# Layer 3's row sums, its last block, and the layout of loads and stores in a four-layer kernel

## The chip, the cores and the metric

The kernel runs on one core of a Trainium2 chip. A core has a matrix engine (TensorE, PE in the profile; its weight loads are listed as PEld), a vector engine (VectorE, DVE), a scalar engine (ScalarE, ACT), a general engine (GpSimd, POOL) and a queue processor (SyncE, SP). TensorE reads the on-chip memory SBUF, which has 128 partitions, and writes the accumulators in PSUM. SP, ScalarE and GpSimd can issue DMAs; these run on 16 DMA engines that all queues share. The metric is the time of one execution on the device in microseconds (us), the median of several runs.

## The reference

The input `x` has four images of 64 x 64 positions with 64 channels, all float32. Four layers follow one another; each keeps the shape.

```python
# layer 0: attention over the 4096 positions of an image, applied transposed
attn = softmax(q @ k.T);  x = gamma * (attn.T @ v) + x
# layer 1: norm, 1x1 conv to 256, 3x3 depthwise conv, y1*y2, channel attention, 1x1 conv, add;
#          norm, 1x1 conv to 256, z1*z2, 1x1 conv, add
# layer 2: x is read as (B, C, H, W) though it is (B, H, W, C); N = 4096
attn = softmax(xf.T @ xf);  x = (xf @ attn.T) + x
# layer 3: attention with 32 inner channels
f = softmax(theta_x @ phi_x.T);  w_y = (f @ g_x) @ w_W + w_b
mean, var = w_y.mean((0, 1, 2)), w_y.var((0, 1, 2))      # over all four images
x = x + gamma * (w_y - mean) * rsqrt(var + 1e-3) + beta
```

Layer 3's softmax needs, for each of 4096 queries, a sum of exponentials over 4096 keys; and its normalisation needs the statistics of all four images before any output can be written.

## The kernel before, in words

`fast_path` does the work; at its end a count of row sums outside a safe range (`bad`) decides whether `general_path` is run instead, and here it isn't.

**Layout.** An image is kept as `X[:, b]`, 128 x 2048: the partition is 64 x (parity of the column) + channel, and the free index runs over 32 column pairs with 64 rows h in each. A load brings rows h into partitions and 128 values (two columns of 64 channels) into each of eight blocks q, then TensorE transposes the blocks (`load_x`, L886). The view of the loads and stores is `by_rows = "h (q p w) c -> p h q (w c)"` (L733): column = 4q + 2p + w, so that one piece that is contiguous in memory is two columns, 512 bytes. Each image takes four loads (`g` and `p`, L744) of 256 KB, all on SP, and four stores (L1445), all on SP.

**Order of the work.** TensorE, ScalarE and VectorE run in an order written out by hand (`tc.manual_schedule`, `run()`). A list `items` holds the score steps, in turn layer 0 of all images (32 items each), then layer 2 of image 0, layer 2 of image 1, layer 3 of image 0, and so on; layer 3 of image 3 (`layer3(B - 1)`) is last. `due` holds what has to follow an item by so many items. Two lanes, `conv` (layer 1) and `misc` (projections, loads, closing steps), put generator steps between the items by a table of estimated times. What stands after `run()`, the normalisation and the stores, isn't under the manual schedule: the scheduler places it, each engine still executing its own list in order.

**Layer 3** handles an image in two halves of 32 items. In item n, `scores` makes a 128-key by 2048-query block of scores with four row groups of TensorE (L1284) into two PSUM tiles, and ScalarE writes the exponentials to `e` (L1289), one of six buffers. Two items later, `products` multiplies `e` by `gx` with four column groups (L1297), and the same `e` is added to the row sums in one of two ways:

```python
            if mc % 10 == 9:
...
                for k in range(4):
                    mm(
                        st["z"][32 * k : 32 * k + 32, :], ones[:, 0:32], e[:, bass.ts(k, 512)],
                        start=mc == 9, stop=False,
                    )
            elif mc == 1:
                nc.vector.tensor_add(esum, es[n - 1], e)
            elif mc:
                nc.vector.tensor_add(esum, esum, e)
```

TensorE sums over the key partitions with a matrix of ones (L1305) for the blocks 9, 19 and 29 of a half, VectorE adds the other blocks elementwise (L1310, L1312). At the end of a half, `totals` brings VectorE's sum through the ones into the same accumulator `z` (L1320), copies `z` to SBUF on ScalarE (L1324), takes its reciprocal (L1325) and scales the products (L1326) on VectorE. `close` multiplies by the output weights (L1336), adds the bias on ScalarE (L1338), gathers statistics in `bst` (L1340) and the extremes of the reciprocals (L1342) for the safe-range check. A float32 matmul stands in the trace as two passes, so a group of four is eight records.

**The end.** After the last half, the statistics are aggregated (L1412); TensorE averages the mean over the two parities with the matrix `half` (L1414), VectorE forms squared differences (L1418 to L1420), TensorE averages these (L1421), and a few one-column instructions give scale and shift (L1423 to L1428). Eight output tiles follow: scale and shift on ScalarE (L1434), add to `X` on VectorE (L1435), eight transposes (L1438), copies by VectorE and ScalarE (L1442, L1443), two stores (L1445). Then the flag `bad` is read by every engine and the kernel closes.

**The start.** While SP loads the images, GpSimd loads the weights, and ScalarE's queue loads 28 small vectors into `rows` and `gam` (L805, L810, L824), which TensorE turns into columns (L816) ahead of the first projection.

Of the kernel before, what the change touches and what calls it, by code (L numbers as in the profile page):

```python
# [691 lines left out]
def fast_path(ctx: ExitStack, tc: tile.TileContext, a: dict, out: bass.AP, bad):  # L692
# [42 lines left out]
    by_rows = "h (q p w) c -> p h q (w c)"  # L735
    rows_x = []
    for b in range(B):
        if b % 2 == 0:
            both = new_big("xr")
        t = both[:, bass.ts(b % 2, 2048)].rearrange("p (q n) -> p q n", n=128)  # L740
        src = a["x"][b].rearrange(by_rows, p=2, w=2)
        for g in range(2):
            for p in range(2):
                nc.sync.dma_start(  # L744
                    out=t[64 * p : 64 * p + 64, bass.ts(g, 8)], in_=src[p, :, bass.ts(g, 8)]
                )
        rows_x.append(t)
# [22 lines left out]
    ones = const.tile([128, 64], F32, name="ones")  # L770
# [109 lines left out]
    bst = const.tile([128, B, 2, 2, 6], F32, name="bst")  # L880
# [176 lines left out]
    def layer1(b):  # L1057
# [5 lines left out]
        for r in (1, 0):  # L1063
# [6 lines left out]
            inner = pad[:, PW + 1 : 65 * PW + 1].rearrange("p (q s h) -> p q s h", s=2, h=PW)  # L1070
            for j in range(4):
# [6 lines left out]
                for s in range(2):  # L1078
                    act(  # L1079
                        inner[:, bass.ts(j, 8), s, 0:H],  # L1080
                        ps[:, bass.ts(s, 512)].rearrange("p (q h) -> p q h", h=H),
                        AF.Identity, bias=pwb[:, 0, r : r + 1],
                    )
# [27 lines left out]
        for j in range(4):  # L1111
            ps = new_ps()
            for s in range(2):
                w0 = 16 * j + s
                mm(
                    ps[64 * s : 64 * s + 64, 0:512], pw2s, yg[:, w0 : w0 + 15 : 2, :],
                    start=True, stop=True,
                )
# [155 lines left out]
    def layer3(b):  # L1274
        m, first = im[b], len(items)
# [15 lines left out]
        def products(n):  # L1291
# [9 lines left out]
            if mc % 10 == 9:  # L1301
                if mc == 9:
                    st["z"] = new_acc("accz")
                for k in range(4):
                    mm(  # L1305
                        st["z"][32 * k : 32 * k + 32, :], ones[:, 0:32], e[:, bass.ts(k, 512)],
                        start=mc == 9, stop=False,
# [9 lines left out]
        def totals():  # L1317
# [6 lines left out]
            nc.scalar.copy(yz[:, 512:1024], z)  # L1324
            nc.vector.reciprocal(yz[:, 512:1024], yz[:, 512:1024])  # L1325
            nc.vector.tensor_mul(yz[:, 0:512], yz[:, 0:512], yz[:, 512:1024])  # L1326

        def close(nb):
# [6 lines left out]
            for jj in range(2):  # L1335
                mm(ps[:, bass.ts(jj, 512)], wo[jj], yz[:, 0:512], start=True, stop=True)  # L1336
            wy = wys[b][:, bass.ts(nb, 1024)]
            act(wy, ps, AF.Identity, bias=V("L3_conv_w_b"))  # L1338
            for i in range(2):
                nc.vector.bn_stats(bst[:, b, nb, i, :], wy[:, bass.ts(i, 512)])  # L1340
# [64 lines left out]
    half = new_t("half")[:, 0:128]  # L1405
    for i in range(2):
        nc.vector.tensor_scalar_mul(half[:, 64 * i : 64 * i + 64], ident[:, 0:64], 0.5)
    for i in range(2):
        cols = slice(64 * i, 64 * i + 64)
        stt(half[:, cols], ident[:, 64:128], 0.5, half[:, cols], ALU.mult, ALU.add)  # L1410
# [3 lines left out]
    mm(ps[:, 0:1], half, mv[:, 0:1], start=True, stop=True)  # L1414
    mean = sm.tile([128, 1], F32, tag="mean", name="mean")
    nc.vector.tensor_copy(mean, ps[:, 0:1])
    dm = sm.tile([128, 1], F32, tag="dm", name="dm")
    nc.vector.tensor_sub(dm, mv[:, 0:1], mean)  # L1418
    nc.vector.tensor_mul(dm, dm, dm)
    nc.vector.tensor_add(dm, dm, mv[:, 1:2])  # L1420
    mm(ps[:, 512:513], half, dm, start=True, stop=True)  # L1421
    scale = sm.tile([128, 1], F32, tag="scale", name="scale")
    act(scale, ps[:, 512:513], AF.Sqrt, bias=eps3)  # L1423
# [3 lines left out]
    nc.vector.tensor_mul(shift, scale, mean)  # L1427
    nc.vector.tensor_sub(shift, V("L3_conv_beta"), shift)  # L1428
    for b in range(B):
        dst = out[b].rearrange(by_rows, p=2, w=2)  # L1430
        for g in range(2):
# [12 lines left out]
            for p in range(2):  # L1444
                nc.sync.dma_start(  # L1445
# [72 lines left out]
```

## Time and profile before

| what | value |
|---|---|
| median of 3 runs | 2860.71 us (2859.96 to 2860.85) |
| the profiled execution: its own time | 2859.4 us |
| its span, first to last instruction | 2857.6 us |
| TensorE busy | 2756.5 us, 96% |
| ScalarE busy | 1751.3 us, 61% |
| VectorE busy | 1443.8 us, 51% |
| ones for row sums, L1305 | 192 records (24 groups) |
| adds for row sums, L1312 and L1310 | 216 x 2.29 us and 8 x 2.29 us |
| loads of x, stores of out | 16 and 16, 256 KB each, 4.7 and 4.6 us to landing |

The profile is one execution of the program. A row of a group of instructions names the line, the engine, the operation, and output and input tiles; "x8" is the number of instructions, and the time beside a row of the order in time is from the first start to the last end. TensorE overlaps its instructions, so the length of one record is more than what it adds to a stream. A wait names the instruction that ended it. The chain lists what ended last, followed back from the end.

### The profile page before, as it was taken

The numbers are of one execution on the slowest core, as the hardware profiler recorded it, in microseconds if no ns is written. First come the engines' busy times: TensorE is split into PE (matmuls) and PEld (weight loads), VectorE is DVE, ScalarE is ACT, GpSimd is POOL, SyncE is SP. The second block draws the span as 40 slices with busy tenths as digits, with TensorE's granted clock in tenths as the row PEclk, the third lists the DMA queues.
The fourth block names the chain that finished last, engine by engine and source line by source line (L and its number), as shares of the span: only waits on it lengthen the run. The fifth ranks groups of instructions, "written<-read, shape, count | busy, mean of one in ns | idle before, by whom it ended". The sixth has DMA issues, their size and how long they took to land.

```text
span 2857.6 us, 41692 instructions
## 1 busy us (share of the span) xinstructions
PE 2756.5 (96%) x17976; PEld 933.6 (33%) x17976; DVE 1443.8 (51%) x1548; ACT 1751.3 (61%) x2815; POOL 25.0 (1%) x85
## 2 busy tenths in 40 slices
PE   6999999999999999989999999999999999999995
PEld 3333333333333333322333332243322333322222
DVE  2322386633875438622673118930058610198996
ACT  3555555556465555655655558855678756578884
POOL 3000000000000000000000000000000000000000
PEclk9999999999999999999999999999999999999997
DMA  3000000000000000000000000000000000000002
GB/s 70 1 1 1 0 1 1 1 0 1 1 1 1 1 0 1 1 1 1 1 1 1 1 1 1 1 1 1 1 1 1 1 1 1 1 1 1 1 1 60
DMA packets 18460, 11.86 MB, mean 4 GB/s; under 512 B 1300, under 2 KB 18141, under 8 KB 18269
## 3 DMA queue, kind: packets, MB, share of 16 engines
q1 hardware_dynamic: 16896, 8.39, 1.4%
q8 instruction: 142, 2.33, 0.3%
q0 software_dynamic: 1120, 0.72, 0.2%
q14 instruction: 49, 0.40, 0.0%
q10 hardware_dynamic: 253, 0.02, 0.0%
HBM read 4.94 MB, written 4.19 MB: 3 GB/s over the span
## 4 chain that ended last, share of the span: by engine, by line
PE 91%; DVE 5%; ACT 3%; issue 1%; POOL 0%; DMA 0%; ACTq 0%; DVEq 0%; POOLq 0%
PE acc L1007 16%; PE ps L983 16%; PE acc L1194 16%; PE ps L1177 15%; PE ps L1284 9%; PE acc L1297 8%; PE ps L1131 2%; PE ps L1074 1%; PE ps L1031 1%; ACT e L1289 1%; DVE yz L1325 1%; PE ps L1336 1%; PE accz L1305 1%; DVE tg L1312 1%; PE var L1040 1%
## 5 line engine op out<-in xcount | busy, mean ns | idle before, releaser
L987 ACT ACTIVATE e<-ps 128x1024 f32<-128x1024 f32 x512 | 516.8, 1025 | 325.2 <-PE ps L983 201.0
L1185 ACT ACTIVATE e<-ps 128x1024 f32<-128x1024 f32 x512 | 517.0, 1024 | 315.4 <-PE ps L1177 314.9
L1289 ACT ACTIVATE e<-ps 128x1024 f32<-128x1024 f32 x512 | 496.1, 1023 | 110.2 <-PE ps L1284 92.4
L1312 DVE TENSOR_TENSOR tg<-tg,e 128x2048 f32<-128x2048 f32 x216 | 495.0, 2292 | 27.2 <-ACT e L1289 8.5
L983 PE MATMUL ps<-kv,q 64*128 64x512 f32 x2048 | 491.4, 607 | 11.9 <-ACT e L987 3.9
L1177 PE MATMUL ps<-ko 64*64 64x512 f32 x4096 | 473.9, 595 | 18.1 <-ACT ko L1160 8.7
L1194 PE MATMUL acc<-e,X 64*64 64x512 f32 x4096 | 467.7, 591 | 0.6 <-ACT yz L1315 0.6
L1007 PE MATMUL acc<-e,vq 128*64 128x512 f32 x2048 | 467.3, 598 | 0.0
L1014 DVE SCALAR_TENSOR_TENSOR X<-acc,gam,X 128x512 f32<-128x512 f32 x256 | 191.3, 749 | 276.8 <-PE acc L1007 263.9
L1284 PE MATMUL ps<-tg,ph 32*128 32x512 f32 x2048 | 320.3, 640 | 5.6 <-ACT e L1289 4.2
L983 PEld LDWEIGHTS ps<-kv,q 64*128 64x128 f32 x2048 | 189.1, 186 | 293.4 <-issue 187.6
L1297 PE MATMUL acc<-e,tg 128*32 128x512 f32 x2048 | 272.7, 605 | 1.3 <-ACT yz L1315 1.3
L1177 PEld LDWEIGHTS ps<-ko 64*64 64x64 f32 x4096 | 152.4, 133 | 313.7 <-issue 196.4
L1194 PEld LDWEIGHTS acc<-e,X 64*64 64x64 f32 x4096 | 156.9, 133 | 281.5 <-issue 271.3
L1007 PEld LDWEIGHTS acc<-e,vq 128*64 128x64 f32 x2048 | 136.3, 136 | 311.9 <-issue 289.9
L1202 DVE TENSOR_TENSOR ph<-ph,acc 128x512 f32<-128x512 f32 x16 | 11.0, 688 | 387.6 <-ACT ph L1201 387.6
L1284 PEld LDWEIGHTS ps<-tg,ph 32*128 32x128 f32 x2048 | 102.3, 183 | 223.6 <-issue 149.0
L1096 DVE SCALAR_TENSOR_TENSOR y<-pad,vec,y 128x1024 f32<-128x1024 f32 x128 | 164.3, 1283 | 7.6 <-ACT pad L1079 3.5
L1096 DVE SCALAR_TENSOR_TENSOR yg<-pad,vec,yg 128x1024 f32<-128x1024 f32 x128 | 164.3, 1284 | 3.8
L987 ACT ACTIVATION_READ_ACCUMULATOR e<-ps 128x1 f32 x512 | 106.5, 208 | 0.0
L1185 ACT ACTIVATION_READ_ACCUMULATOR e<-ps 128x1 f32 x512 | 105.9, 207 | 0.0
L1297 PEld LDWEIGHTS acc<-e,tg 128*32 128x32 f32 x2048 | 41.0, 108 | 196.4 <-issue 190.6
(173 smaller groups left out, 1229.2 us busy)
## 6 DMA issues: line engine op xcount, KB each, us to landing
xr<-in_x_dram SPq DMA_DIRECT2D x16, 256.0 KB, 4.7
out_dram<-o SPq DMA_DIRECT2D x16, 256.0 KB, 4.6
pw<-in_L_conv_pw_w_dram POOLq DMA_DIRECT2D x4, 64.0 KB, 4.2
phw<-in_L_conv_phi_W_dram POOLq DMA_DIRECT2D x8, 8.0 KB, 3.7
wq<-in_L_conv_Wq_dram POOLq DMA_DIRECT2D x4, 16.0 KB, 6.6
sca<-in_L_conv_sca_w_dram POOLq DMA_DIRECT2D x1, 64.0 KB, 3.8
pw<-in_L_conv_pw_w_dram POOLq DMA_DIRECT2D x2, 32.0 KB, 4.0
thw<-in_L_conv_theta_W_dram POOLq DMA_DIRECT2D x4, 8.0 KB, 3.7
```

What stands on the lines that cost most here:

```text
L983: mm(ps[:, bass.ts(r, 512)], m.q[rows_, bass.ts(t, 128)], m.k[rows_, bass.ts(g, 512)], start=True, stop=True,)
L987: act(es[g // 2][:, bass.ts(g % 2, 1024)], ps, AF.Exp, bias=SHIFT0, accum_out=zs[:, g : g + 1],)
L1007: mm(accs[g][64 * r : 64 * r + 64, :], vq, es[half][:, 1024 * g + 512 * r : 1024 * g + 512 * r + 512], start=t == 2 * p, stop=t == 2 * p + 1,)
L1014: stt(xs, accs[g], gam0, xs, ALU.mult, ALU.add)
L1096: stt(out_, win, wt, out_, ALU.mult, ALU.add)
L1177: mm(ps[64 * c : 64 * c + 64, bass.ts(r, 512)], m.ko[rows_, 128 * jb + 64 * c : 128 * jb + 64 * c + 64], m.ko[rows_, bass.ts(2 * ib + r, 5 ...
L1185: act(es[n, jb], ps, AF.Exp, bias=SHIFT2, accum_out=m.zs[:, jb, ib : ib + 1])
L1194: mm(acc[r][64 * c : 64 * c + 64, :], xw[rows_, jb, :], es[n, jb][rows_, bass.ts(c, 512)], start=jb == 0, stop=jb == 31,)
L1284: mm(tiles[k // 2][:, bass.ts(k % 2, 512)], m.ph[rows_, bass.ts(mc, 128)], m.th[rows_, bass.ts(nb, 512)], start=True, stop=True,)
L1289: act(e[:, bass.ts(kp, 1024)], tiles[kp], AF.Exp)
L1297: mm(st["y"][32 * k : 32 * k + 32, :], m.gx[:, mc, :], e[:, bass.ts(k, 512)], start=mc == 0, stop=mc == 31,)
L1312: nc.vector.tensor_add(esum, esum, e)
```

## The change

The diff has five parts.

- **Row sums.** A half's blocks 5, 11, 17, 23 and 29 go to TensorE's ones in place of 9, 19 and 29; in the last image's second half the blocks 30 and 31 (items 62 and 63) go there too.
- **The closing of a half.** Reciprocal and multiply are done in two pieces of 256 columns; the output matmul, the bias and the statistics follow by pieces as well, so that `bst` has twice the entries. For the last image the reciprocal reads the accumulator in PSUM directly, with no copy by ScalarE.
- **The statistics.** The variance over the two parities comes from half their sum and half their difference: `half` gets a second part, two matmuls are issued together, and the second round of TensorE is left out.
- **Layout.** The column is 32p + 2q + w, so that eight blocks q of one p are contiguous in memory, 4 KB for each row h. The depthwise convolution needs the true column order, so the writes into `pad` (L1079) and the reads of `yg` (L1115) are permuted. The other layers treat positions alike whatever their order.
- **Stores.** Those of p = 0 stay on SP, those of p = 1 are issued from GpSimd.

```diff
--- before.py
+++ after.py
@@ -732,13 +732,13 @@
 
 
     X = keep.tile([128, B, 2048], F32, name="X")
-    by_rows = "h (q p w) c -> p h q (w c)"
+    by_rows = "h (p q w) c -> p h q (w c)"
     rows_x = []
     for b in range(B):
         if b % 2 == 0:
             both = new_big("xr")
         t = both[:, bass.ts(b % 2, 2048)].rearrange("p (q n) -> p q n", n=128)
-        src = a["x"][b].rearrange(by_rows, p=2, w=2)
+        src = a["x"][b].rearrange(by_rows, p=2, q=16)
         for g in range(2):
             for p in range(2):
                 nc.sync.dma_start(
@@ -767,7 +767,7 @@
     nc.gpsimd.memset(eps1, EPS1)
     eps3 = const.tile([128, 1], F32, name="eps3")
     nc.gpsimd.memset(eps3, EPS3)
-    ones = const.tile([128, 64], F32, name="ones")
+    ones = const.tile([128, 32], F32, name="ones")
     nc.gpsimd.memset(ones, 1.0)
 
     def blocks(nm, weight, n_out, places, width):
@@ -877,7 +877,7 @@
     sums0 = const.tile([128, B, 32], F32, name="sums0")
     sums2 = const.tile([128, B, 32], F32, name="sums2")
     ext3 = const.tile([128, B, 2, 2], F32, name="ext3")
-    bst = const.tile([128, B, 2, 2, 6], F32, name="bst")
+    bst = const.tile([128, B, 2, 4, 6], F32, name="bst")
 
     def load_x(b):
         for g in range(2):
@@ -1067,7 +1067,7 @@
             nc.gpsimd.memset(
                 pad[:, PW : 65 * PW].rearrange("p (w h) -> p w h", h=PW)[:, :, 0:1], 0.0
             )
-            inner = pad[:, PW + 1 : 65 * PW + 1].rearrange("p (q s h) -> p q s h", s=2, h=PW)
+            inner = pad[:, PW + 1 : 65 * PW + 1].rearrange("c (p q s h) -> c q p s h", p=2, s=2, h=PW)
             for j in range(4):
                 ps = new_ps()
                 for s in range(2):
@@ -1077,8 +1077,8 @@
                     )
                 for s in range(2):
                     act(
-                        inner[:, bass.ts(j, 8), s, 0:H],
-                        ps[:, bass.ts(s, 512)].rearrange("p (q h) -> p q h", h=H),
+                        inner[:, bass.ts(j, 4), :, s, 0:H],
+                        ps[:, bass.ts(s, 512)].rearrange("c (q p h) -> c q p h", p=2, h=H),
                         AF.Identity, bias=pwb[:, 0, r : r + 1],
                     )
                 yield 3.5
@@ -1111,9 +1111,9 @@
         for j in range(4):
             ps = new_ps()
             for s in range(2):
-                w0 = 16 * j + s
                 mm(
-                    ps[64 * s : 64 * s + 64, 0:512], pw2s, yg[:, w0 : w0 + 15 : 2, :],
+                    ps[64 * s : 64 * s + 64, 0:512], pw2s,
+                    yg.rearrange("c (p q s) h -> c q p s h", p=2, s=2)[:, bass.ts(j, 4), :, s, :],
                     start=True, stop=True,
                 )
             t = new_t()
@@ -1272,7 +1272,7 @@
         yield 3.5
 
     def layer3(b):
-        m, first = im[b], len(items)
+        m, first, last = im[b], len(items), b == B - 1
         es, st = {}, {}
 
         def scores(n):
@@ -1298,13 +1298,13 @@
                     st["y"][32 * k : 32 * k + 32, :], m.gx[:, mc, :], e[:, bass.ts(k, 512)],
                     start=mc == 0, stop=mc == 31,
                 )
-            if mc % 10 == 9:
-                if mc == 9:
+            if mc % 6 == 5 or (last and n >= 62):
+                if mc == 5:
                     st["z"] = new_acc("accz")
                 for k in range(4):
                     mm(
                         st["z"][32 * k : 32 * k + 32, :], ones[:, 0:32], e[:, bass.ts(k, 512)],
-                        start=mc == 9, stop=False,
+                        start=mc == 5, stop=False,
                     )
             elif mc == 1:
                 nc.vector.tensor_add(esum, es[n - 1], e)
@@ -1321,9 +1321,13 @@
                     z[32 * k : 32 * k + 32, :], ones[:, 0:32], m.tg[:, 2048 + 512 * k : 2560 + 512 * k],
                     start=False, stop=True,
                 )
-            nc.scalar.copy(yz[:, 512:1024], z)
-            nc.vector.reciprocal(yz[:, 512:1024], yz[:, 512:1024])
-            nc.vector.tensor_mul(yz[:, 0:512], yz[:, 0:512], yz[:, 512:1024])
+            if not last:
+                nc.scalar.copy(yz[:, 512:1024], z)
+                z = yz[:, 512:1024]
+            for i in range(2):
+                cols, inv = bass.ts(i, 256), slice(512 + 256 * i, 768 + 256 * i)
+                nc.vector.reciprocal(yz[:, inv], z[:, cols])
+                nc.vector.tensor_mul(yz[:, cols], yz[:, cols], yz[:, inv])
 
         def close(nb):
             yz = st["yz"]
@@ -1332,12 +1336,20 @@
             if nb == 0:
                 wys[b] = wys["pair"][:, bass.ts(b % 2, 2048)]
             ps = new_ps()
-            for jj in range(2):
-                mm(ps[:, bass.ts(jj, 512)], wo[jj], yz[:, 0:512], start=True, stop=True)
-            wy = wys[b][:, bass.ts(nb, 1024)]
-            act(wy, ps, AF.Identity, bias=V("L3_conv_w_b"))
             for i in range(2):
-                nc.vector.bn_stats(bst[:, b, nb, i, :], wy[:, bass.ts(i, 512)])
+                cols = bass.ts(i, 256)
+                for jj in range(2):
+                    mm(
+                        ps[:, 512 * jj + 256 * i : 512 * jj + 256 * i + 256], wo[jj], yz[:, cols],
+                        start=True, stop=True,
+                    )
+                wy = wys[b][:, bass.ts(nb, 1024)].rearrange("p (j n) -> p j n", j=2)[:, :, cols]
+                act(
+                    wy, ps.rearrange("p (j n) -> p j n", j=2)[:, :, cols], AF.Identity,
+                    bias=V("L3_conv_w_b"),
+                )
+                for jj in range(2):
+                    nc.vector.bn_stats(bst[:, b, nb, 2 * i + jj, :], wy[:, jj, :])
             for i, op in enumerate((ALU.max, ALU.min)):
                 nc.vector.tensor_reduce(ext3[:, b, nb, i : i + 1], yz[:, 512:1024], AX.X, op)
 
@@ -1402,32 +1414,31 @@
         run()
 
 
-    half = new_t("half")[:, 0:128]
-    for i in range(2):
-        nc.vector.tensor_scalar_mul(half[:, 64 * i : 64 * i + 64], ident[:, 0:64], 0.5)
-    for i in range(2):
-        cols = slice(64 * i, 64 * i + 64)
-        stt(half[:, cols], ident[:, 64:128], 0.5, half[:, cols], ALU.mult, ALU.add)
+
+    half = new_t("half")[:, 0:256]
+    for i in range(4):
+        nc.vector.tensor_scalar_mul(half[:, bass.ts(i, 64)], ident[:, 0:64], 0.5)
+    for i in range(4):
+        cols = bass.ts(i, 64)
+        stt(half[:, cols], ident[:, 64:128], -0.5 if i > 1 else 0.5, half[:, cols], ALU.mult, ALU.add)
     mv = sm.tile([128, 2], F32, tag="mv", name="mv")
     nc.vector.bn_aggr(mv, bst.rearrange("p b n i s -> p (b n i s)"))
     ps = new_ps()
-    mm(ps[:, 0:1], half, mv[:, 0:1], start=True, stop=True)
-    mean = sm.tile([128, 1], F32, tag="mean", name="mean")
-    nc.vector.tensor_copy(mean, ps[:, 0:1])
-    dm = sm.tile([128, 1], F32, tag="dm", name="dm")
-    nc.vector.tensor_sub(dm, mv[:, 0:1], mean)
-    nc.vector.tensor_mul(dm, dm, dm)
-    nc.vector.tensor_add(dm, dm, mv[:, 1:2])
-    mm(ps[:, 512:513], half, dm, start=True, stop=True)
+    mm(ps[:, 0:2], half[:, 0:128], mv, start=True, stop=True)
+    mm(ps[:, 512:513], half[:, 128:256], mv[:, 0:1], start=True, stop=True)
+    mean = sm.tile([128, 4], F32, tag="mean", name="mean")
+    nc.vector.tensor_copy(mean[:, 0:2], ps[:, 0:2])
+    nc.vector.tensor_copy(mean[:, 2:3], ps[:, 512:513])
+    stt(mean[:, 3:4], mean[:, 2:3], mean[:, 2:3], mean[:, 1:2], ALU.mult, ALU.add)
     scale = sm.tile([128, 1], F32, tag="scale", name="scale")
-    act(scale, ps[:, 512:513], AF.Sqrt, bias=eps3)
+    act(scale, mean[:, 3:4], AF.Sqrt, bias=eps3)
     nc.vector.reciprocal(scale, scale)
     nc.vector.tensor_mul(scale, scale, V("L3_conv_gamma"))
     shift = sm.tile([128, 1], F32, tag="shift", name="shift")
-    nc.vector.tensor_mul(shift, scale, mean)
+    nc.vector.tensor_mul(shift, scale, mean[:, 0:1])
     nc.vector.tensor_sub(shift, V("L3_conv_beta"), shift)
     for b in range(B):
-        dst = out[b].rearrange(by_rows, p=2, w=2)
+        dst = out[b].rearrange(by_rows, p=2, q=16)
         for g in range(2):
             cols = bass.ts(g, 1024)
             xs, ws = X[:, b, cols], wys[b][:, cols]
@@ -1442,7 +1453,7 @@
             nc.vector.tensor_copy(o[:, 0:512], ps[:, 0:512])
             nc.scalar.copy(o[:, 512:1024], ps[:, 512:1024])
             for p in range(2):
-                nc.sync.dma_start(
+                (nc.gpsimd if p else nc.sync).dma_start(
                     out=dst[p, :, bass.ts(g, 8)],
                     in_=o[64 * p : 64 * p + 64, :].rearrange("p (q n) -> p q n", n=128),
                 )
```

## The prediction

> **What bounds the kernel now.** I read the page's engine totals, TensorE's waits, a table of windows over layer 3, the order in time on TensorE, the chain at the end, and last the DMA waits.
>
> ```profile
> span 2857.6 us, 41692 instructions
> PE 2756.5 (96%) x17976; PEld 933.6 (33%) x17976; DVE 1443.8 (51%) x1548; ACT 1751.3 (61%) x2815; POOL 25.0 (1%) x85
> ```
>
> TensorE is busy 96% of the span. Layer 3 runs four times in two halves of 32 key blocks; the windows below are three of those eight halves, and the sum covers all eight.
>
> ```profile
> 2574.00:2650.00 76.00, 75.00 (x552) 19.55 (x548) 65.68 (x33) 63.75 (x68) 0.00 (x0) 1.00 0.00 1
> 2650.00:2727.00 77.00, 76.00 (x560) 19.86 (x556) 71.48 (x36) 64.46 (x68) 0.00 (x0) 1.00 0.00 1
> 2727.00:2803.00 76.00, 75.00 (x552) 19.49 (x548) 70.01 (x34) 63.93 (x67) 0.00 (x0) 1.00 0.00 1
> sum 617.00, PE 609.07 PEld 162.84 DVE 539.31 ACT 503.25 POOL 0.00; mean PE 76.13 PEld 20.36 DVE 67.41 ACT 62.91 POOL 0.00
> ```
>
> The columns are length, then PE, PEld, DVE, ACT. VectorE is close (70 of 76), but TensorE is bound: 609 of 617, so at most 8 us of stalls could ever be given back. One group of ones, among its neighbours:
>
> ```profile
> 2624.03 1.06 PE L1297 MATMUL acc<-e,tg 128*32 128x512 f32 x8
> 2625.02 1.25 PE L1284 MATMUL ps<-tg,ph 32*128 32x512 f32 x8
> 2626.20 1.06 PE L1297 MATMUL acc<-e,tg 128*32 128x512 f32 x8
> 2627.09 1.04 PE L1305 MATMUL accz<-e,ones 128*32 128x512 f32 x8
> 2628.06 1.14 PE L1284 MATMUL ps<-tg,ph 32*128 32x512 f32 x8
> 2629.13 1.06 PE L1297 MATMUL acc<-e,tg 128*32 128x512 f32 x8
> ```
>
> From products to products is 2.17 us (2624.03 to 2626.20) without the ones and 2.93 with them; over the pairs of blocks around, 4.31 against 5.17. A group costs TensorE 0.86 us. The chain at the end, where TensorE has run dry:
>
> ```profile
> 2807.96 2.30 DVE tg L1312
> 2810.30 1.98 PE accz L1320 x8
> 2812.30 0.59 ACT yz L1324
> 2812.92 3.36 DVE yz L1325
> 2817.15 3.77 PE ps L1336 x4
> 2820.93 1.12 ACT wy L1338
> 2822.08 1.29 DVE bst L1340 x2
> 2823.37 1.18 DVE ext L1342 x2
> ```
>
> The last products end at 2804.6; VectorE, behind by then, ends its sums at 2810.26. Everything is serial until the shift at 2828.53; then eight output tiles, the last copied at 2846.13, and 16 stores from one queue, issued until 2851.89. At the start:
>
> ```profile
> PE ps L816 <- DMA rows<-in_L_conv_phi_b_dram: 21.9, 1, 21.9
> ```
>
> TensorE's first real work (24.5 us) waits for the last of 28 small vector loads on ScalarE's queue.
>
> **The skill.** TensorEngine Tiling (Array Packing), Key Properties, says that a change of tiling mode drains TensorE. This trace agrees: scores and products are four passes of 0.43 us, 1.72, yet a block takes 2.155; a ones group keeps the products' mode and pays only its two passes, 0.86. TensorE: Matmul & The Clock Gate, Part 1, says that an idle window of about 3.4 us halves the clock. The trace agrees: the granted clock is 0.50 from 2812, after the 5.7 us wait, and L1336's four records take 3.77 where they take 1.92 mid-kernel. DMA: Bandwidth & Descriptors gives 408.7 GB/s for loads in 4 KiB rows from SP (iDMA fabric), and says that several issuing engines save issue time only (Issuing engines are not separate DMA queues). Here 512 B packets make 153 to 164 GB/s over the two DMA phases; nothing here shows 4 KB from HBM at rest.
>
> **The change, part by part.**
>
> 1. *More sums on TensorE.* Ones at five blocks of 32 instead of three: 2 x 8 halves = 16 groups x 0.86 = **+13.8** (0.80 to 1.07, the row's own length, a group: 12.8 to 17.1). VectorE loses 16 adds of 2.39 (2.29 and gap), but they are no bound, so 38 us freed there return little. The stall between adjoining halves (ScalarE waits 2 us for L1310 to free an exponential buffer, TensorE about 1.8) stems from the reciprocal ahead of L1310, which stays. I credit 1 us where image 3's projections share the first half of layer3(2), and 1 us between image 3's halves, where the reciprocal no longer waits for the copy behind ScalarE's exponentials: **-2** (bounds 0 and -6).
> 2. *Halved closes* in the seven earlier halves: 8 records of 256 columns for 4 of 512, the same streaming, hidden if weights (0.19) load under 0.215 of streaming; +0.1 each. Two halved reciprocals and multiplies add about 0.15 of fixed VectorE time, which delays L1310, and the scores behind it, in four places. No gain is possible, since instructions are only added: **+1** (0 to +3). Where the last image's reciprocal reads `accz` itself, that buffer stays taken some 4 us longer; the next sums want it at block 5, 8 us on.
> 3. *The tail.* After the products of block 61 with its ones (2800.94, as now) follow y and ones of 62 and 63, and the totals at once, since the last add is block 60's: seven groups x 0.86 + 0.3 of fill = 2807.3, against 2812.24: **-5**, the two extra groups (1.7) included. From there to the aggregate's end is 12.8 now (2825.04). After: no ScalarE copy; reciprocal half 1.71 + multiply 0.43, twice, 4.3; the second half's matmuls 1.0 at full clock or 1.9 at half, I take 1.6; activation 0.65, two statistics 0.75, extremes 1.2, aggregate 0.7 (twice the entries; 0.58 now), gaps 0.3. Sum 9.5: **-3.3**. Statistics to shift: one matmul round (0.6) and three small VectorE operations go, a second matmul's weight loads and two operations come: **-0.8** (0 to -1.2). The four extra operations on the `half` matrix take 0.2 each while VectorE waits for the totals; uncovered they cost 0.8. Bounds of the three together, with the clock full or half throughout and each gap doubled or gone: -7 to -11.
> 4. *Stores.* The tiles' pace stays, 1.74 us each (0.69 + 1.22 on VectorE, overlapped). The SP queue spends 1.07 per store, so the last issue trails the last copy by 5.8. With eight stores on each queue and 4 KB runs the issue follows the copies: 256 KB at 408.7 GB/s is 0.64, an estimate from the DMA page's figure. SP would then finish 5 to 6 earlier. But GpSimd closes with work of its own: in the trace its closing semaphore instruction takes 0.9 and its drain 2.92, now hidden under SP's stores. With stores on its queue, that and its load of the flag stand behind the last store and its landing: copy 2846.2, issue 0.55, landing 2.3 to 3, then 0.3 + 0.9 + 2.9, then the final barrier 0.9: about 2854.0 against 2857.6: **-3.6** (-6 if the drain shrinks, 0 if landing is as slow as the 6 us seen in the loads).
> 5. *Loads.* Queue starts on SP and ScalarE share semaphores: ScalarE's vector loads start at 5.28, 6.61, 7.97 and 10.78 as the image loads land, then follow at 0.61 each to 20.98; the last lands 3.5 later. Image loads land 1.35 apart (256 KB, 194 GB/s). At 300 GB/s, between this and the page's 408.7, five of them save 2.5, and the last small load lands in a quieter queue, 0.5: **-3** (-5.3 at 408.7 with a landing of 2; 0 if the rate holds; +1 if small packets queue behind long ones). GpSimd's weights must then not be later: pw3 is issued by 15.96 and lands about 4 later, early enough.
> 6. *The permuted writes* into `pad` (L1079), and `yg`'s reads, keep elements and counts. A convolution's first block now needs three fills, not two; the waits show only 3.5 us behind such fills, all on VectorE, which has slack in layer 1. Zero; a late VectorE would cost one fill spacing, 3.5 us of VectorE per pad, and TensorE's own wait before L1115 is 1.4 in all.
>
> Sum: +13.8 - 2 + 1 - 5 - 3.3 - 0.8 - 3.6 - 3 = **-2.9**. The profiled execution took 2859.4 (span 2857.6), the median of the runs is 2860.7, so 2860.7 - 2.9 = **2857.8 us**. Within 0.2%, 5.7 us, this kernel can't tell a change from none.
>
> **Rivals.**
>
> *A, as summed: 2858.* Chance 0.42, own range 2854 to 2862.
>
> *B, the ends pay in full: 2851.* Loads -5.3, stores -6, stalls -4, where A has -3, -3.6, -2: 6.7 more, so -9.6. For it: both DMA phases are saturated (nine tenths busy). Against: GpSimd's drain, and ScalarE's 0.61 per issue, which the length of the runs doesn't touch. Chance 0.30.
>
> *C, slower: TensorE's clock.* The trace shows six single windows at half clock before the tail, each 3.41 long, so 1.7 lost; two of them follow the stall between halves (L1336 takes 3.62 and 3.27 instead of 1.92). There are five such stalls, and the two-step close lengthens each. One more at each of the three not hit now, and three beside the stalls on ScalarE in layers 0 and 2, where four occur now, cost 6 x 1.7 = 10.2: 2868. It decides from two windows more (+3.4). Against: 0.15 longer is little. Chance 0.15.
>
> *D, the runs stay at 512 B* because the copies keep eight pieces per partition: loads 0, stores -1: +2.7, 2863.4. Against: both sides are contiguous over those pieces in the new layout. Chance 0.13.
>
> **Numbers.** Faster than 2855.0 is most of B (0.28) and an edge of A (0.05): 0.33. Slower than 2866.4 is most of C (0.12) and a part of D, if its stores are late too (0.05): 0.17. The rest is 0.50. The range holds A, D and most of B and reaches to C's near side: 2850 to 2867.
>
> **What would show it.** L1305 at 336 records where it has 192 (24 groups become 42); halves 1.7 longer with VectorE near 60 of 78; no wait at L1320; the reciprocal reading `accz` within 0.2 of L1320's end; x packets of 4 KB or so and L816 near 21.5; the last store landing about 3 after the last copy, GpSimd's drain after it. I am wrong if the halves grow less than 1 us (VectorE was the bound), if L816 stays at 24.5, or if half-clock windows become frequent.

## The result and the profile after

The changed kernel takes 2872.93 us in the median (2872.23 to 2873.36), the kernel before, on the same chip, 2860.34. The ratio is 1.0045, 95% interval [1.0028, 1.0063]: it is **slower by about 12.6 us**. The forecast was 2857.8 with a range up to 2867. The profiled execution took 2872.96.

The page of the changed kernel, its span and the engines' busy times:

```profile
span 2871.1 us, 42034 instructions
PE 2773.0 (97%) x18152; PEld 940.9 (33%) x18152; DVE 1406.2 (49%) x1565; ACT 1756.0 (61%) x2821; POOL 29.4 (1%) x93
```

VectorE has lost 38 us of work and TensorE has gained 16.5, and the span has grown by 13.5. Where, is told by the starts of the first and last scores of each stage. Half clock is the time for which the trace grants TensorE 0.5, in windows of 3.4 us; one such window costs up to 1.7.

| stretch | before | after | difference |
|---|---|---|---|
| start to the first scores (L983) | 41.50 | 39.66 | -1.8 |
| layers 0 to 2, to layer 3's first scores | 1659.52 (13.7 at half clock) | 1663.89 (17.1) | +4.4 |
| layer 3, first to last scores (L1284) | 1099.41 (6.8) | 1119.97 (3.4) | +20.6 |
| last scores to the end | 57.20 | 47.55 | -9.7 |

Layer 3 is the loss. These are the windows of its last three halves after the change, with the columns as in the table of before (length, PE, PEld, DVE, ACT):

```profile
2588.70:2668.30 79.60, 77.21 (x576) 20.79 (x572) 66.22 (x37) 64.12 (x69) 0.00 (x0) 1.00 0.00 1
2668.30:2747.80 79.50, 77.11 (x573) 20.69 (x569) 66.13 (x37) 64.04 (x69) 0.00 (x0) 1.00 0.00 1
2747.80:2822.90 75.10, 73.70 (x550) 19.88 (x546) 64.70 (x42) 60.77 (x66) 0.00 (x0) 1.00 0.00 1
```

A half between two others has gone from 76.2 to 79.5. Two groups of ones account for 1.7 of that. The other 1.66 lies in one place, the close of the half before. Here is that place in time, from the last scores ahead of a close on, first before the change (in TensorE's order), then after:

```profile
2592.14 1.13 PE L1284 MATMUL ps<-tg,ph 32*128 32x512 f32 x4 [0.73 <-ACT e L1289]
2593.19 1.99 PE L1336 MATMUL ps<-yz,wo 128*128 128x512 f32 x4
2595.11 1.06 PE L1297 MATMUL acc<-e,tg 128*32 128x512 f32 x8
```

```profile
2686.37 1.13 PE L1284 MATMUL ps<-tg,ph 32*128 32x512 f32 x4 [0.99 <-ACT e L1289]
2687.43 1.13 PE L1342 MATMUL ps<-yz,wo 128*128 128x256 f32 x4
2688.93 0.71 ACT L1347 ACTIVATE wy<-ps,vec 128x512 f32<-128x512 f32 x1
2689.69 1.13 PE L1342 MATMUL ps<-yz,wo 128*128 128x256 f32 x4 [1.13 <-ACT wy L1347]
2690.76 0.64 PE L1297 MATMUL acc<-e,tg 128*32 128x512 f32 x4
```

Before, four matmuls run through in 1.92 us (2593.19 to 2595.11). After, the first half's matmuls are followed by ScalarE's activation of that half, and only when it has ended do the second half's matmuls start: 3.33 us (2687.43 to 2690.76). A bracket gives the wait and its releaser. Both halves write one PSUM tile, `ps`, which the activation reads. The columns that the second pair writes (256 to 511 and 768 to 1023) are none of those that the activation reads (0 to 255 and 512 to 767), and it waits all the same. The scores ahead of the close wait 0.99 us for ScalarE where they waited 0.73.

The end of the kernel went as forecast. The order of VectorE and TensorE there, where before stood the chain from L1312 to L1342:

```profile
2829.22 1.04 PE L1320 MATMUL accz<-tg,ones 128*32 128x512 f32 x8
2830.33 1.76 DVE L1329 RECIPROCAL yz<-accz 128x256 f32<-128x256 f32 x1 [7.02 <-PE accz L1320]
2832.53 1.75 DVE L1329 RECIPROCAL yz<-accz 128x256 f32<-128x256 f32 x1
2834.89 1.10 PE L1342 MATMUL ps<-yz,wo 128*128 128x256 f32 x4 [1.09 <-DVE yz L1330]
2838.60 1.01 DVE L1425 BATCH_NORM_AGGREGATE mv<-bst 128x2 f32<-128x192 f32 x1
```

Nothing waits for VectorE's sums at L1320 any more. From the last scores to the totals' end it is 6.1 us (11.2 before), from there to the aggregate's end 9.35 (12.8), on to the first scaled tile 2.9 (3.5). But from the last copied tile to the end it is 11.6, as before (11.5).

At the start, the wait that carries it is 2.7 us shorter (21.9 before). The projections at L941 then give 0.9 back: they take 4.62 us for 3.71. The trace's record of full clock begins at 29.7 us, 1.9 after their start; until then pairs of them come 0.85 to 1.0 apart, afterwards 0.43. Before the change it begins just as they start.

```profile
PE ps L816 <- DMA rows<-in_L_conv_phi_b_dram: 19.1, 1, 19.1
```

### The profile page after: what moved, and what is told of

Its sections match the earlier page's. It is cut to its first block, busy times and chain, and to the rows that moved or that the text cites. A ratio compares the mean times of both kernels' runs of the same rounds, so it can differ in the third digit from the quotient of the medians.

```text
span 2871.1 us, 42034 instructions
## 1 busy us (share of the span) xinstructions
PE 2773.0 (97%) x18152; PEld 940.9 (33%) x18152; DVE 1406.2 (49%) x1565; ACT 1756.0 (61%) x2821; POOL 29.4 (1%) x93
## 3 DMA queue, kind: packets, MB, share of 16 engines
HBM read 4.94 MB, written 4.19 MB: 3 GB/s over the span
## 4 chain that ended last, share of the span: by engine, by line
issue 50%; PE 46%; DVE 2%; ACT 1%; DMA 0%; ACTq 0%; POOL 0%; SPq 0%; POOLq 0%; DVEq 0%
PE acc L1007 16%; PE ps L983 16%; PE acc L1194 4%; PE ps L1177 4%; PE ps L1131 1%; PE ps L1074 1%; PE ps L1031 1%; PE ps L954 1%; PE var L1040 0%; PE ps L960 0%; PE ps L1049 0%; DVE yg L1096 0%; PE ps L941 0%; PE ps L1114 0%; PE ps L1141 0%
## 5 line engine op out<-in xcount | busy, mean ns | idle before, releaser
L983 PE MATMUL ps<-kv,q 64*128 64x512 f32 x2048 | 491.9, 606 | 11.9 <-ACT e L987 3.8
L1312 DVE TENSOR_TENSOR tg<-tg,e 128x2048 f32<-128x2048 f32 x198 | 453.7, 2291 | 50.5 <-ACT e L1289 36.0
L1284 PE MATMUL ps<-tg,ph 32*128 32x512 f32 x2048 | 319.4, 640 | 5.0 <-ACT e L1289 4.5
L983 PEld LDWEIGHTS ps<-kv,q 64*128 64x128 f32 x2048 | 188.1, 186 | 295.3 <-issue 185.2
L1284 PEld LDWEIGHTS ps<-tg,ph 32*128 32x128 f32 x2048 | 101.8, 182 | 222.3 <-issue 133.8
```

The costliest lines, as they stand in the source:

```text
L983: mm(ps[:, bass.ts(r, 512)], m.q[rows_, bass.ts(t, 128)], m.k[rows_, bass.ts(g, 512)], start=True, stop=True,)
L1284: mm(tiles[k // 2][:, bass.ts(k % 2, 512)], m.ph[rows_, bass.ts(mc, 128)], m.th[rows_, bass.ts(nb, 512)], start=True, stop=True,)
```

## The experiments

All figures are medians beside runs of the kernel before, which had 2859.3 to 2859.6 in these series. Times of one version spread over about 10 us here, and the number of half-clock windows differs between executions; so stretches of the traces are compared as well. A stretch net of half-clock windows has half of their length, 1.7 us a window, taken off. The combined version, named before its own section, has the shortened end and the new layout, with all stores on SyncE, three groups of ones in a half and whole closes in the seven earlier halves.

### The close: whole, or with two PSUM tiles

The first run closes seven halves in one piece, reciprocals, matmuls and activation, and leaves only the last halved. From the close's loop:

```diff
-            for i in range(2):
-                cols = bass.ts(i, 256)
+            width = 256 if last and nb == 1 else 512
+            for i in range(512 // width):
+                cols = bass.ts(i, width)
```

> The changed kernel with the close in one piece in seven of the eight halves: the reciprocals, the output matmuls and the ScalarE activation take 512 columns at once again, and only the last image's second half is still halved; the pieces of bn_stats stay 256 columns wide. Theory 1 (the halved close holds TensorE, 1.3 to 1.7 us in each of the seven earlier halves): 9.5 to 11.5 us less than the changed kernel, about 2862.5, and the gap between the two groups of scores around the close of the second halves falls from 8.35 to about 6.7 us. Rival (the halves are as good as hidden, and layer 3's growth is ones groups and clock windows alone): 0 to 2 us less, about 2872.

Measured: 2862.66 (2856.39 to 2865.77, 14 runs), ratio to before 1.0011 [1.0003, 1.0019]. Layer 3 takes 1108.76 in place of 1119.97, **11.2 us less**, with the same 3.4 us at half clock, and the gap at the close (from the start of the last group of scores ahead of it to the start of the next group) is 6.68 us in place of 8.35. Theory 1 holds: the halved closes cost 1.6 us in each of seven halves. The median is 3.4 us above the kernel before; the changed kernel's is 12.6 above, and 15.9 in a later series.

The second run keeps the halves and gives each its own tile:

```diff
-            ps = new_ps()
             for i in range(2):
+                ps = new_ps()
```

> The changed kernel with each half of a close in its own PSUM tile, so that the second half's output matmuls need not wait until ScalarE has read the first half. Theory 1a (the shared tile is what holds TensorE): 7 to 9 us less, about 2865, and the second pair of output matmuls follows the first without a wait for ScalarE. Rival (the close costs what it does because ScalarE has one more activation in its queue and TensorE waits for its exponentials): 0 to 2 us less, about 2872.

Measured: 2867.1 (2859.75 to 2869.3), ratio 1.0020 [1.0008, 1.0031]. TensorE at one close of this run:

```profile
2685.07 1.99 PE L1342 MATMUL ps<-yz,wo 128*128 128x256 f32 x8
2686.99 1.07 PE L1297 MATMUL acc<-e,tg 128*32 128x512 f32 x8
```

The eight small matmuls run through in 1.92, exactly as the four large ones did before, without waiting for ScalarE. The gap at undisturbed closes falls from 8.35 to 6.95: of the 1.67 us of a close, 1.40 is the wait on the shared tile. Layer 3, net of half-clock windows, is 9.5 us shorter than in the changed kernel; seven times 1.40 is 9.8. At two closes of the profiled execution (8.60 and 8.59) a half-clock window stands on top, 1.65 each. That execution, 2869.3, is the slowest of the seven; that windows also keep the median above the theory's 2865 is not shown. The rival, ScalarE's queue, can have at most the remaining 0.27. This is the longer wait of the scores ahead of the close: it is 0.99 in this run too, and 0.73 again with whole closes. That points to the halved reciprocals and multiplies, which only the first run makes whole.

### The groups of ones

```diff
-            if mc % 6 == 5 or (last and n >= 62):
-                if mc == 5:
+            if mc % 10 == 9 or (last and n >= 62):
+                if mc == 9:
```

> The changed kernel with the groups of ones at blocks 9, 19 and 29 of each half again, and the two extra ones at the last image's blocks 30 and 31 kept: 16 groups fewer on TensorE, 16 additions of 2.29 us more on VectorE. Theory 1 (TensorE pays the whole of a group, 0.82 to 0.86 us): 13 us less, about 2860. Rival (VectorE then falls behind around the closes and gives 4 to 6 us of it back): 8 us less, about 2865.

Measured: 2864.49 (2861.71 to 2868.96), ratio 1.0021 [1.0012, 1.0030], 8.4 us less than the first series of the changed kernel, which is the rival's number. Its mechanism does not show: the undisturbed close between the last two images takes 7.49 us, which is the 5.83 of before and 1.66 for the halves, and TensorE waits nowhere for VectorE's sums at L1320. Three other closes take 9.72 to 9.95, with 6.8 us of half clock at each, 2.2 to 2.5 longer; in this execution they can account for what is missing from 13. A clean price of the ones comes from the combined version below: its layer 3 takes 1096.27, the version with whole closes 1108.76, with the same half clock, and up to the end of layer 3 they differ in 16 groups of ones alone. That is 12.5 us, 0.78 a group.

Fewer groups than before were tried from the other side, in the combined version: two (`mc in (10, 21)`), and one (`mc == 15`).

> The combined version (shortened end, 4 KB layout, stores on SyncE) with two groups of ones in each half, at blocks 10 and 21, in place of three. Theory (TensorE pays 0.86 for a group and VectorE, with 29 additions of 2.29 us in a half of 73, still keeps up): 0.86 x 8 = 6.9 us less than the combined version. Rival (VectorE is full around the closes, as its stall of 1.4 there in the kernel before shows, and each addition more is paid there): 0 to 2 us less.

> The combined version with one group of ones in each half, at block 15. Theory: 13.8 us less than the combined version, if VectorE keeps up with 30 additions (68.7 us of a half's 71.5). Rival: VectorE becomes the bound of the half, and the time is that of the combined version or above it.

Measured: 2852.12 (ratio 0.9971 [0.9960, 0.9982]) with two and 2866.36 (1.0022 [1.0016, 1.0029]) with one, against 2847.93 with three, on another chip (the kernel before took 2859.39 on this one, 2859.55 on that). Both theories fail. With one group the rival holds. With two the rival has the cause, VectorE, but not the size: 4.2 us more, where it said 0 to 2 less. TensorE's wait at the totals, first with two groups, then with one:

```profile
PE accz L1320 <- DVE tg L1312: 10.3, 5, 2.8
```

```profile
PE accz L1320 <- DVE tg L1312: 23.8, 6, 5.3
```

With two groups the first halves of the first two images do become 0.8 shorter (74.25 for 75.04), as TensorE's price says. But at the end of five halves, the second of every image and the last image's first, VectorE is late with its sums, and TensorE waits for them at L1320 (1.3 to 2.8 each, 10.3 in all). With one group it waits 23.8 in all. With three groups the matmuls at L1320 have no such wait in the combined version's trace, so that two more cost TensorE time and save it none. Of one, two, three and five groups, three is the fastest, the number of the kernel before; four was not tried.

### Stores

> The changed kernel with all sixteen stores issued by SyncE, none by GpSimd. Theory (the 4 KB rows did shorten the transfers by 4 us, and GpSimd's wait for landing, its semaphore step and its drain at the end, some 3.6 us more than SyncE's, took it back): 3 to 4 us less, about 2869.3, with 2 to 3 us from the last packet to the end instead of 6.0. Rival (one queue issues the sixteen too slowly, or the two queues are what made the transfers shorter): the transfers take 20 us again and the time is 2873 or more.

```diff
-                (nc.gpsimd if p else nc.sync).dma_start(
+                nc.sync.dma_start(
```

Measured: 2869.13 (2866.04 to 2873.83, 5 runs), ratio 1.0037 [1.0024, 1.0051]. The issues to the output in the changed kernel, and in this one (queue, count, size, us from issue to landing):

```profile
out_dram<-o SPq DMA_DIRECT2D x8, 256.0 KB, 5.1
out_dram<-o POOLq DMA_DIRECT2D x8, 256.0 KB, 4.9
```

```profile
out_dram<-o SPq DMA_DIRECT2D x16, 256.0 KB, 4.1
```

From the last copied tile to the end it is 10.1 with one queue, 11.6 with two, 11.5 before the change. Two queues shorten the transfers, first packet to last, from 16.2 to 15.4 us (19.1 with the old rows; in the combined version only from 16.6 to 16.5), but after the last packet comes 5.8 us in place of 3.2. The trace's records show what fills it: after its stores have landed, GpSimd takes 1.05 for a semaphore step and then 3.57 for a drain, until 2870.24, while SyncE has been done since 2867.39. The median is 3.8 us below the first series of the changed kernel, as the theory says, but the stretch that it speaks of gives 1.5 in the trace: it holds in kind, and the other 2.3 are not traced to the stores.

The same two queues were put into the combined version:

> The combined version with each tile's second store issued by GpSimd, as in the changed kernel. Theory (GpSimd's closing steps cost more than its queue wins): 1.5 to 2.5 us more than the combined version, about 2849.8, with about 6 us from the last packet to the end instead of 2.5. Rival (the two queues are worth their price here): the same or less.

Measured: 2849.38 (2845.74 to 2850.75) against 2847.93 (2843.37 to 2848.09, on another chip): 1.5 us more, as the theory says, but the ranges overlap and the medians alone don't decide. In the traces, last packet to end is 6.1 and 2.5, last copy to end 13.4 and 9.9.

### The layout alone, and where layers 0 to 2 grew

The layout edits of the diff (`by_rows`, loads, `inner`, `yg`'s columns, `dst`) in the kernel before, all stores on SyncE:

> The kernel before with the 4 KB layout alone: loads, padded image, projections' columns and stores by the new order, all stores on SyncE, the rest as before. The prediction's sum would give 3 for the loads and 3.6 for the stores, 6 to 6.6 us less than before. Theory 2 (as the changed kernel's traces read: 1.8 at the loads and 1.4 at the stores without GpSimd, but about 2.6 back in layers 0 to 2, whose stretch up to layer 3's first scores was 1655.3 us in three of the runs against 1652.7 before, once 1.7 is taken off for each window of half clock): 0.5 to 1 us less, within the uncertainty. Rival 2 (that stretch grew by chance, in windows alone): 3.2 us less.

Measured: 2855.65 (2851.03 to 2859.27, 21 runs), ratio 0.9982 [0.9976, 0.9989]: 3.9 us less, more than theory 2 says and nearer rival 2. The trace of this run, however, shows what theory 2 names: start 39.44 (-2.1), last copy to end 10.2 (-1.3), and layers 0 to 2 1655.4 net of half-clock windows (each counted as 1.7) against 1652.7 (+2.7), with 17.1 us at half clock for 13.7. The net figure is good to about 0.5: it is 1654.5 to 1655.4 in the twelve traces with the new layout, and 1652.6 in the shortened end alone, which has the old one. Most times lie in two groups, about 2851.5 and 2857.3, with three between, and the profiled execution was of the upper one. By the trace the layout gives 0.7; the rest of the medians' difference would then lie in the windows. The place where the windows differ, in the combined version's profiled execution (2843.37) and in the layout alone (the eighth column, after the five engines, is the granted clock):

```profile
990.00:1006.00 16.00, 12.38 (x43) 4.59 (x40) 4.92 (x9) 7.67 (x13) 0.00 (x0) 0.89 0.00 0
```

```profile
990.00:1006.00 16.00, 12.37 (x30) 3.57 (x28) 2.80 (x4) 6.90 (x11) 0.00 (x0) 0.68 0.00 0
```

With the same layout, this stretch once has one window and once three. A second run of the layout alone:

> The layout alone, a second look: its times lay in two groups, about 2851.5 and 2857.3, and the first look (2857.8) had 17.1 us of half clock in layers 0 to 2. Theory (the groups differ by three windows of half clock near 995 and 1640 us, 1.7 each): with 2851 to 2852 there are 7 us of half clock in that stretch, with 2857 to 2858 there are 17. Rival (the difference lies at the stores or elsewhere): 17 us in both.

It took 2855.12, between the groups, with 10.2 us at half clock in that stretch (1660.51 long, 1655.4 net). So windows move the time within a version, and the net figure stays. That they make the two groups in full is not shown.

What the net 2.7 is was tried in the kernel before, first by the order of the pad's writes alone:

```diff
-                        inner[:, bass.ts(j, 8), s, 0:H],
-                        ps[:, bass.ts(s, 512)].rearrange("p (q h) -> p q h", h=H),
+                        inner[:, bass.ts(j, 8), s, 0:H].rearrange("p (b a) h -> p a b h", b=2),
+                        ps[:, bass.ts(s, 512)].rearrange("p (b a h) -> p a b h", b=2, h=H),
```

> The kernel before, with the 64 writes of layer 1's padded image in an order of three dimensions in place of two: the same rows to the same places, the rows of each job taken as 4 by 2 instead of 0 to 7. Theory (in the new layout each such write takes 0.70 us for 0.64 because of its third dimension, and TensorE's next scores wait behind it in ScalarE's queue): the write takes 0.70, layers 0 to 2 up to layer 3's first scores grow by 2 to 3 us net of half-clock windows, and the time is about 2862. Rival (the growth of 2.7 there comes from the layout's other order of rows, for which the first depthwise step waits): the same time as before, and 1652.7 us net in that stretch.

Measured: 2859.95, ratio 1.0003 [0.9995, 1.0011], and 1654.05 net in layers 0 to 2: +1.4, half of the 2.7. Neither expectation holds as stated: the stretch grows, but the write itself does not become slower (medians 0.689 and 0.694 us). ScalarE at one pair of these writes, before the change and in the changed kernel:

```profile
348.18 1.27 ACT L1079 ACTIVATE pad<-ps,pwb 128x512 f32<-128x512 f32 x2 [2.79 <-PE ps L1074]
349.34 1.02 ACT L987 ACTIVATE e<-ps 128x1024 f32<-128x1024 f32 x1
```

```profile
346.41 1.42 ACT L1079 ACTIVATE pad<-ps,pwb 128x512 f32<-128x512 f32 x2 [2.70 <-PE ps L1074]
347.72 1.01 ACT L987 ACTIVATE e<-ps 128x1024 f32<-128x1024 f32 x1
```

The pair takes 1.42 for 1.27. In the records the second write of a pair starts 585 ns after the first in the kernel before, overlapping it by 0.1 us; in the changed kernel and in this experiment it waits on a semaphore that the first one raises, and starts 722 to 723 ns after it. The exponential behind the pair, and TensorE's next scores, come later by that 0.14.

Then also the third fill of the pad that the new order asks of the first 16-row window (`for j in (1, 0, 2, 3)` in the convolution), with those writes and without:

> The kernel before with the three-dimensional pad writes, and with the convolution's 16-row windows taken in the order 1, 0, 2, 3, so that the first of them needs three fills of the pad, as in the new layout, and not two. Theory (the layout's 2.7 us in layers 0 to 2 is 1.4 for the writes and 1.3 for VectorE's later start on each pad): 1655.3 us net of half-clock windows in that stretch, with VectorE waiting some 7 us for the fills. Rival (the remaining 1.3 is something else of the layout): 1654.0 net, as with the writes alone.

> The kernel before with the windows' order 1, 0, 2, 3 alone, the pad writes as before. Theory: 1654.0 us net in layers 0 to 2 (1652.7 and 1.3). Rival: 1652.7.

Measured: 2858.89 (ratio 0.9997 [0.9988, 1.0006]) and 1654.2 net; alone 2857.88 in one run and 1653.0 net. VectorE does wait 7.3 and 7.0 us for the fills, as in the changed kernel, but TensorE's stretch grows by 0.2 to 0.3 only. The rival held. Of the 2.7, about 1.6 is explained so; 1.1 stays open.

### The end alone, and the combined version

The kernel before with the edits of the last half and of the statistics, nothing else:

> The kernel before with the shortened end alone: ones groups for the last image's blocks 30 and 31, the last half closed in halves, the last image's totals read from PSUM, the statistics in one step; ones groups elsewhere at blocks 9, 19 and 29, the other seven halves closed whole, the old layout, all stores on SyncE. Theory 1 (the end's three steps do as forecast, and all that was lost lies in the ones groups and the halved closes): 8 to 9 us less than before. Rival (the end's gain needs the extra ones groups of the whole image, or waits for VectorE's additions again): 4 us less or smaller.

Measured: 2849.32 (2846.78 to 2854.03), ratio 0.9969 [0.9957, 0.9980]: **10.2 us less than before**, more than theory 1's 8 to 9. Totals, aggregate and first tile stand at the distances of the changed kernel (1.72 from the last products to the totals, 9.35, 2.86). Layer 3 is 1.4 shorter besides, since the last image's first close no longer waits for ScalarE's copy (gap 4.42 for 5.83).

With the layout as well:

> The shortened end and the 4 KB layout together, all stores on SyncE, without the additional ones groups and with seven halves closed whole. Theory 2: 9 to 10 us less than before, that is 0 to 1 less than the shortened end alone. Rival 2 (the layout is worth 3.2 or more by itself): 12 us less or more.

Measured: 2847.93 (2843.37 to 2848.09, 5 runs), ratio 0.9957 [0.9944, 0.9970]: **11.6 us less than before**, between the two expectations and nearer the second, and 25.0 and 27.5 less than the changed kernel in its two series. It beats both kernels; from the end alone its interval doesn't part it.

The changed kernel itself, beside these:

> The changed kernel unchanged, so that the versions beside it have it on the same chip. Every theory: about 12 us above the kernel before.

Measured: 2875.45 (2866.87 to 2876.52), ratio 1.0046 [1.0034, 1.0058]: 15.9 us above the kernel before, where about 12 was expected. Four of its six times lie at 2875.1 to 2876.5, two at 2866.9 and 2869.0.

## Why the prediction was wrong

The sum said -2.9, the spans say +13.5. Step by step, with what the runs put in place of each term:

- **Halved closes, +1: this step failed, and by itself it is enough to turn the sign.** It measured 11.2. The price of the instructions was right (eight small matmuls stream as four large ones do, 1.92). What was left out is the order that the loop makes: matmuls, activation, matmuls, on one tile. The second pair has to wait until ScalarE has read the first, 1.40 us, and behind it wait the scores of a TensorE that was busy 99% of layer 3. The remaining 0.27 a close fits the delay by the halved reciprocals, which the forecast had, at 0.15 and in four places. The line "hidden if weights (0.19) load under 0.215 of streaming" looked at TensorE alone. The bound of 3 for this edit was no bound, for the same reason. With seven closes whole again the time is 2862.66, inside the forecast's range.
- **Ones +13.8 and relief -2: right.** 16 groups cost 12.5 in the combined comparison, just under the forecast's bound of 12.8, and the copy's absence between the last image's halves gave 1.4, where 1 was credited; the other credit of 1 was not measured by itself. Layer 3 without the closes grew by 20.6 - 11.2 = 9.4, or 11.1 when the one half-clock window that before had more is put back; forecast 11.8.
- **The end, -5 - 3.3 - 0.8: right.** 5.1, 3.4 and 0.6 in the trace, and by itself worth 10.2 in the medians with the relief of 1.4. The 3.4 depends on the clock: in the combined version's execution, where the closing matmuls ran at half clock, the same steps gave 1.9.
- **Stores, -3.6: failed.** It came to +0.1. The rows alone give 1.1 to 2.0 over six traces, and the transfers did become shorter, 19.1 to 15.4. The forecast took a store's landing as 2.3 to 3 and it is 5; GpSimd's closing steps (0.9 + 2.9 in the forecast, 1.05 + 3.57 after) then stand uncovered behind it. The mechanism was named; its size was set at the good end although the bound of 0 stood beside it.
- **Loads, -3: the right way, too large.** 1.8 in the changed kernel and 2.1 with the layout alone; over all traces the first scores start at 40.5 to 41.7 us with the old rows and at 38.5 to 40.6 with the new. The early image loads land 1.13 us apart, 232 GB/s, where the working took 300 between 194 and the 408.7 that the Trainium skill gives (DMA: Bandwidth & Descriptors, iDMA fabric), there for DMAs of 1 MiB. No run here comes near that figure. The small loads on ScalarE's queue are 21 in the trace and in the code, not 28 as stated.
- **Permuted writes, 0: failed by 2.7.** Counts and elements are the same, as said; but the second write of each pair now waits for the first, which accounts for 1.4; 1.1 stays open. The third fill, which the forecast had weighed, costs TensorE next to nothing, as it said.

Half-clock windows don't explain the sign: the profiled execution has one more than before in layers 0 to 2 and one fewer in layer 3. The rival of clock windows had forecast 2868, the nearest of the four, by a mechanism that is not the one at work; the time went to a wait on a shared tile that no rival named. Taken together: -2.9, +10.2 (closes), +3.7 (stores), +2.7 (writes), +1.2 (loads), -1.3 (ones and end, with 0.5 less over the output tiles) gives +13.6.

## What to carry to other kernels

Splitting a step in halves can pay where the engines around it have run dry: at the very end the halves and the dropped copy together saved 3.4 us here. In the seven earlier halves the same lines cost 1.6 each, mostly because a bound TensorE was made to wait in the middle for a reader of its own tile. When a loop of matmul and activation is cut in pieces, read which tile the next piece writes and who still reads it; a tile for each piece took most of that price away here. A `ps` laid out so that each half has a 512-column part to itself was not tried. A second engine's DMA queue brings its own closing work, so count that from its last landing, not only the issues it saves.

## What was not expected of the hardware

- The end of a program with stores on GpSimd's queue takes 5.8 to 6.2 us from the last packet, with SyncE alone 2.3 to 3.2.
- Two ScalarE activations in a row with no semaphore between them start 585 ns apart though each lasts 689; with a semaphore between them 722 to 723.
- Stores of 4 KB rows over one queue move 4.19 MB in 16.2 us, 259 GB/s, over two in 15.4, 273 GB/s, and 512 B rows in 19.1, 220 GB/s: eight times the row gains a fifth. These are whole stretches, in which the output tiles come one after another; the other traces have 16.5 to 17.1, 15.4 to 16.5 and 19.0 to 19.2 us.
- A window of half clock stood at some closes and not at others of one and the same execution (gaps of 8.60 and 6.95 with two PSUM tiles), though TensorE had waited 0.99 us ahead of each. What decides it stays open.
